# A planned two-layer metaformer kernel: layer 0's projection weights get a tile of their own, weights lie in one run a partition, and the planner lets ScalarE's and GpSimd's instructions overlap

## The chip, the cores and the metric

The kernel runs on one core of one Trainium2 chip. The metric is the device time of one execution in microseconds (us), the median of several runs. TensorE (PE) multiplies matrices, VectorE (DVE), ScalarE (ACT) and GpSimd (POOL) work element by element, and SyncE (SP) issues most of the DMAs. Each engine takes its instructions strictly in order; an instruction that waits holds up everything behind it on its engine, SP's DMA requests included.

## The reference

The input is x, 4 images of 384 channels and 32x32 positions, in float32. Two layers follow, and each has a mixing part and a feed-forward part around residual additions (cut from the reference):

```
# layer 0
x = x + L0_conv(ln_c(x))     # selective scan in 4 directions (k = 0..3)
t = tokens(x);  t = t + L0_ffn(ln_t(t))     # low-rank (Kronecker) feed-forward
# layer 1
x = x + L1_conv(ln_c(x))     # Mamba block: in_proj, causal conv of 4 taps, scan, gate, out_proj
t = tokens(x);  t = t + L1_ffn(ln_t(t))     # 4 experts, the best 2 of each token
```

A selective scan computes for each channel d and each of its 16 states n, along the positions:

```
h = exp(dt * A[d, n]) * h + dt * u * B[n]
y = sum over n of  h * C[n]
```

`dt`, `B` and `C` come from a small projection of the scan's own input. In layer 0 that projection has the weights `x_proj_weight`, 44 columns for each of the 4 directions; the kernel calls them `w_x0`. In layer 1 it is `w_x1` with 56 columns.

## The kernel before

**Scan steps.** Half an image (512 positions) in one direction, or in one half of layer 1's channels, is a pass. There are 48 passes and each has 12 steps, so 576 steps. A step covers four tiles of 128x512. For each step ACT writes the four decays `exp(dt*A)` into PSUM tiles `da` (`decay`, L1773), POOL multiplies `dt*u` by B into the tile `s` (`times_b`, L1767, one instruction of 128x2048), DVE runs four scans (`scan`, L1782), and the product with C is divided between DVE (`times_c`, L1831, one 128x512 tile each, out of PSUM) and POOL (`times_c_pool`, L1847, the last one or two tiles at once, which the scan then leaves in `s`). PE adds the states up (`add`, L1803), and after four steps DVE gathers the sum (`gather0`, L660 to L666, `gather1`, L913). There are four `s` tiles in rotation (`NSR = 4`).

**Around the scans** run the side jobs: layer norms (`layernorm`, L445 to L476), the projection of a scan's input (`prep_quad0`, L638 for layer 0, `prep_quad1`, L894 for layer 1; each serves two passes and is called a quad), the step sizes of a pass (`prep_pass`, with the stores `dts<-tmp` of L510), layer 0's feed-forward (`post0`: L710, L743, L774), layer 1's input projection and convolution (`prep1`: L793, L832), the output projection (`post1`, L952), the routing (`front`, L1070), the experts (`experts`: L1414, L1436) and the combination (`combine`: L1557, L1607). When the last scan is through, what is left of the experts runs alone; that stretch is called the tail below.

**The order is made by a planner**, the class `Plan`, when the program is built. Each piece of work states its engine and a cost in us (`yield PE, 3.2`), a DMA its engine SP and the time to its landing, `land(kb)`, which is 3.5 us and the kilobytes through 200. The planner keeps for each engine when it will be free (`free`) and for each piece when it will be done (`end`), takes the piece that can begin first by rules of `choose`, and emits its instructions. So a cost in the text moves instructions on all engines, though the chip then runs them as fast as it can. An SP request counts as 0.1 us of SP. The planner also decides, step by step, how many of the four C products DVE takes (`split`): it compares when POOL must begin the next `times_b` (`due_b`) with when it is free. Where PE has a hole in the plan, `fill` puts dummy matmuls there (L1822, 32x256).

**Tiles.** Weights of the side jobs go through four shared tiles `wts` of 128x384 (`wts.take()`, `wts.give()`). Layer 0's quad takes one of them, asks for its `w_x0` (L630) and for the `dt` weights (L631), waits in the plan for the landing and then places its matmuls:

```
wx = yield from wts.take()
yield SP, land(66)
nc.sync.dma_start(out=wx[:, :, : QROW + R0], in_=ins["w_x0"][k].rearrange("(c p) m -> p c m", p=P))
```

A quad's job begins when the quad before it is planned, and the pass that is third before its own first pass (`("pass", p - 3)`). The last thing that a pass issues is the store of `dt*u` (L510, four requests).

Of the kernel before, what the change touches and what calls it, by code (L numbers as in the profile page):

```python
# [18 lines left out]
P = 128  # L19
# [109 lines left out]
SLACK = ({PE: 0.0, DVE: 0.0, ACT: 0.0, POOL: 0.0, SP: 0.0}, {PE: 0.0, DVE: 0.0, ACT: 0.0, POOL: 0.0, SP: 0.0})  # L129
LAG = 0.15  # L130


# [32 lines left out]
class Plan:  # L165
# [66 lines left out]
    def run(self):  # L232
        while True:
# [28 lines left out]
            if isinstance(what, Lane):  # L262
                cost = what.want[1]
                self.free[e] = start + (0.1 if e == SP else cost)
                what.end = start + cost
                what.want = None
                Free.clock = what.end
                what.go(what.end, start)
            else:
                k, op = what  # L270
                self.at[e, k] += 1
                self.free[e] = start + (0.1 if e == SP else op.cost)
                self.end[op.key] = start + op.cost
                op.emit()
# [3 lines left out]
def layers(ctx, tc, ins, out, const):  # L278


    nc = tc.nc
    pvt, ident, mean_w = const["pv"], const["ident"], const["mean_w"]
    eps5, eps6, one, nil, mid = (const["few"][:, i : i + 1] for i in range(5))
    x_in = ins["x"]

# [35 lines left out]
    t1 = Free(tiles(6, [P, T], "t1"))  # L321
    wts = Free(tiles(4, [P, NC, P], "w"))


# [5 lines left out]
    slots = {u: wp.tile([P, 2, NK], I32, name=f"slot{u[0]}{u[1]}") for u in gates}  # L330
    nexts = tiles(2, [P, NE], "next", pool=wp)
    tables = [wp.tile([1, 2, pairs + lones], I32, name=f"table{s}") for s, (_, _, pairs, lones) in enumerate(STAGES)]
    since = wp.tile([P, NE], F32, name="since")
    sels = tiles(2, [P, NK + 1, NE], "sel", pool=wp)
# [60 lines left out]

    out_d = dram.tile([P, NI, D], F32, name="out_d")
    taps_d = dram.tile([NI, P, 4 * P], F32, name="taps_d")
# [82 lines left out]
    def wload(src):  # L480

        w = yield from wts.take()
        yield SP, land(192)
        nc.sync.dma_start(out=w, in_=src)
        return w
# [139 lines left out]
    def prep_quad0(q, b, k):  # L625
        def gen():
            u = st[("u0", b)]
            wx = yield from wts.take()
            yield SP, land(66)
            nc.sync.dma_start(out=wx[:, :, : QROW + R0], in_=ins["w_x0"][k].rearrange("(c p) m -> p c m", p=P))  # L630
            nc.sync.dma_start(out=dtw[dt_rows(q), :], in_=ins["w_dt0"][k])  # L631

            px = yield from ps.take(True)
            yield PE, 3.2
            for pieces in zip(*(in_order(px[h * HP : h * HP + QROW + R0], u, k, h) for h in range(NT))):
                for c in range(NC):
                    for to, of in pieces:
                        nc.tensor.matmul(  # L638
                            to, lhsT=wx[:, c, : QROW + R0], rhs=of[:, c], start=c == 0, stop=c == NC - 1
                        )  # L640
            wts.give(wx)
            for h in range(NT):
                yield ACT, 0.6
                nc.scalar.copy(xd[q["at"] : q["at"] + QROW + R0, cols(h)], px[h * HP : h * HP + QROW + R0])
            rows_out(q, slice(0, L))
            ps.give(px)

        return gen

    def prep_pass0(v, p):  # L650
# [17 lines left out]
    def post0(b, h):  # L668
# [52 lines left out]
        def ffn(lane):  # L721
            def gen():
# [6 lines left out]
                for i in range(2 * lane, 2 * lane + 2):  # L729
                    w, proj1 = yield from wts.two()  # L730
                    yield SP, land(192)
                    nc.sync.dma_start(
# [3 lines left out]
                        out=proj1[:, :, :32],  # L736
                        in_=ins["w_proj1"][i * NC * P : (i + 1) * NC * P].rearrange("(f p) i -> p f i", p=P),
                    )
# [26 lines left out]
        def ffn_out():  # L765
            zg, g = st["zg", b], st["g", b, h]
            spread = yield from wts.take()
            yield SP, land(192)
            of = spread_d.unsqueeze(0).to_broadcast([4, QP, D])
            nc.sync.dma_start(out=spread.rearrange("p a m -> p (a m)"), in_=of)  # L770
            for c in range(NC):
                ph = yield from ps.take()
                yield PE, 1.1
                nc.tensor.matmul(ph, lhsT=spread[:, c, :], rhs=g, start=True, stop=True)  # L774
                yield DVE, 0.65
                nc.vector.tensor_tensor(y[:, c], y[:, c], ph, ALU.add)
# [10 lines left out]

    w_in = ins["w_in"].rearrange("(c p) m -> p c m", p=P)
    w_out = out_d
# [5 lines left out]
    def prep1(b, h):  # L795
# [6 lines left out]
        def conv(i):  # L802
            def gen():
                for j in range(NC):
                    c = i * NC + j
                    w = yield from wload(w_in[:, :, c * P : (c + 1) * P])
                    tile_x = yield from tmp.take()
# [3 lines left out]
                    taps = [dg[:, tap * P : (tap + 1) * P] for tap in range(4)]  # L811
                    t_taps = yield SP, land(256)
                    nc.sync.dma_start(out=dg, in_=taps_d[c])
# [33 lines left out]
        def gate(i):  # L847
            def gen():
                z = yield from tmp.take()
                for j in range(NC):  # L850
                    at = (NI + i * NC + j) * P
                    w = yield from wload(w_in[:, :, at : at + P])
# [28 lines left out]
    def prep_quad1(q, b, h):  # L881
        def gen():
            wx = yield from wts.take()
            wx1 = wx.rearrange("p a m -> p (a m)")[:, : NI * (QROW + R1)].rearrange("p (c m) -> p c m", c=NI)
            yield SP, land(120)
            nc.sync.dma_start(out=wx1, in_=ins["w_x1"].rearrange("(c p) m -> p c m", p=P))
            load_dtw(q, 0)
# [27 lines left out]
    def post1(b, h, early=False):  # L915
# [23 lines left out]
        def project():  # L939
            o = st["o", b, h] = yield from tmp.take()  # L940
            for m in range(NC):
                w = yield from wts.two()
                yield SP, land(384)
                for i in range(2):
                    nc.sync.dma_start(out=w[i], in_=w_out[:, i * NC : (i + 1) * NC, m * P : (m + 1) * P])
                yield from till(lambda: all(("gated", b, h, i) in plan.end for i in range(2)))
# [57 lines left out]
    def centre():  # L1004
# [20 lines left out]
        for i in range(2):  # L1025
# [12 lines left out]
            yield SP, land(576)  # L1038
            nc.sync.dma_start(out=out_d[:, i * NC : (i + 1) * NC], in_=w)
            tmp.give(t)  # L1040
# [13 lines left out]
    def front(u):  # L1054
# [3 lines left out]
        def gen():  # L1058
# [7 lines left out]
            raw = pg[:, 192 : 192 + NK * NG1].rearrange("p (j e) -> p j e", e=NG1)  # L1066
            yield PE, 2.9
            for j in range(NK):
# [94 lines left out]

            yield PE, 1.2
            flat = sel.rearrange("p j e -> p (j e)")
# [348 lines left out]
    def combine(u):  # L1514
# [9 lines left out]
        def some(j):  # L1524
            def gen():
# [24 lines left out]
                for k in range(2):  # L1550
                    nc.scalar.activation(diag[k], ident, AF.Copy, scale=gks[u][:, k, j : j + 1])
                yield PE, 2.0, max(t + 6.0, plan.now + 1.0)
                for c in range(NC):
# [445 lines left out]
def metaformer_kernel(ctx: ExitStack, tc: tile.TileContext, ins, out):  # L1999
# [5 lines left out]
    make_identity(nc, ident)  # L2005
    mean_w = cp.tile([P, P], F32, name="mean_w")
    nc.vector.memset(mean_w, 1.0 / D)
    few = cp.tile([P, 8], F32, name="few")
    for i, x in enumerate((1e-5, 1e-6, 1.0, 0.0, 1.5)):
        nc.vector.memset(few[:, i : i + 1], x)  # L2010
    const = {"pv": pvt, "ident": ident, "mean_w": mean_w, "few": few}
    with tc.manual_schedule():
# [3 lines left out]
def _laid_out(a):  # L2016
# [12 lines left out]
    def reordered(w, rank):  # L2029

        parts = [w[..., rank + NS :, :], w[..., rank : rank + NS, :], w[..., :rank, :]]
        return np.swapaxes(np.concatenate(parts, axis=-2), -1, -2)

    pv = {
# [20 lines left out]
        "pv": np.concatenate([pv[n] for n in _PV], axis=1),  # L2055
        "w_x0": reordered(a["L0_conv_x_proj_weight"], R0),
        "w_dt0": np.swapaxes(a["L0_conv_dt_projs_weight"], 1, 2),
        "w_fc1": a["L0_ffn_c_fc_1"].T,
        "w_proj1": a["L0_ffn_c_proj_1"].T,
# [3 lines left out]
        "w_in": a["L1_conv_in_proj_w"].T,  # L2063
        "w_x1": reordered(a["L1_conv_x_proj_w"], R1),
        "w_dt1": a["L1_conv_dt_proj_w"].T,
# [27 lines left out]
```

## Time and profile before

| | us |
|---|---|
| median of 3 runs | 5031.1 (5026.45 to 5036.6) |
| the profiled execution | 5048.5 |
| its span, first instruction to last | 5046.8 |

| stretch of the span | length | PE busy | DVE busy | ACT busy | POOL busy |
|---|---|---|---|---|---|
| start, 0 to 101 | 101 | 92.3 | 32.8 | 46.4 | 10.7 |
| scan steps, 101 to 4462 | 4361 | 3676.3 | 4084.1 | 2772.0 | 3924.3 |
| tail, 4462 to 5047 | 585 | 554.0 | 43.7 | 223.4 | 43.2 |

A group line of the profile names the source line, the engine, the operation, the tiles (written<-read), the shapes and the count; after the bar come the busy time in us, the mean duration of one in ns, the idle time of the engine just before these instructions, and what ended most of it. In a line of waits the three numbers are the us in total, the times and the longest. In a timeline the first two columns are the start and the length in us; what stands in brackets is the engine's idle time before it and what ended it. An fp32 matmul shows as two records. PEclk is the granted TensorE clock as a share of full speed. Consecutive instructions of DVE, ACT and POOL overlap by some hundredths of a us in the records.

### The profile page before, as it was taken

The page shows a single profiled execution, that of the slowest core. Times are in us where ns is not written, and L with a number is a line of the kernel's source. Part 1 is how long each engine was busy: PE and PEld are TensorE (multiplying, and loading weights), DVE is VectorE, ACT ScalarE, POOL GpSimd, SP SyncE. Part 2 cuts the span into 40 slices and gives each one's busy share as a digit, 9 for nine tenths or more (in the row PEclk, how much of TensorE's full clock was granted, in tenths as well). Part 3 has the DMA queues.
Part 4 walks back from the last instruction along what each step waited for, and adds up shares of the span by engine and source line. Part 5 has one row for each costly group of instructions (what it writes and reads, how often), then busy time and mean ns, then how long its engine had stood idle before and what let it go on. Part 6 is the DMA issues. An engine that isn't in the chain of part 4 may idle for free. (4 is left out here: it accounts for less than half of the span.)

```text
span 5046.8 us, 58008 instructions
## 1 busy us (share of the span) xinstructions
PE 4322.5 (86%) x18375; PEld 2232.8 (44%) x18375; DVE 4160.7 (82%) x5795; ACT 3041.7 (60%) x4769; POOL 3978.1 (79%) x1821
## 2 busy tenths in 40 slices
PE   8877788877777899898878888889888898999997
PEld 3222222223233454344444554344533244679994
DVE  4999999989999899999998999989999899940002
ACT  4545467755544677777655577767786656644441
POOL 2999998889988888999988988989999888930002
PEclk9888898988888899999987899899998998999997
DMA  4345656643443565566655655555655456655554
GB/s 148 110 160 173 196 185 213 203 164 127 150 147 113 193 199 177 166 205 210 198 189 194 214 175 180 156 181 197 220 193 197 151 189 203 202 188 182 167 171 142
DMA packets 438163, 899.38 MB, mean 178 GB/s; under 512 B 74609, under 2 KB 187233, under 8 KB 419425
## 3 DMA queue, kind: packets, MB, share of 16 engines
q1 hardware_dynamic: 380640, 704.28, 43.3%
q10 hardware_dynamic: 49024, 166.22, 9.7%
q0 software_dynamic: 8192, 25.17, 1.5%
q8 instruction: 146, 2.39, 0.2%
q14 instruction: 161, 1.31, 0.1%
HBM read 712.11 MB, written 183.40 MB: 177 GB/s over the span
## 5 line engine op out<-in xcount | busy, mean ns | idle before, releaser
L1767 POOL TENSOR_TENSOR s<-dtus,bt 128x2048 f32<-128x2048 f32 x576 | 2607.2, 4536 | 149.9 <-PE acc L1803 81.8
L1773 ACT ACTIVATE da<-dts,a 128x512 f32<-128x512 f32 x2304 | 1529.5, 686 | 873.5 <-DVE s L1831 778.8
L1847 POOL TENSOR_TENSOR s<-s,ct 128x512 f32<-128x512 f32 (+1 forms) x547 | 911.8, 1668 | 162.7 <-DVE s L1782 118.6
L1831 DVE TENSOR_TENSOR s<-da,ct 128x512 f32<-128x512 f32 x1558 | 1029.6, 680 | 0.0
L1803 PE MATMUL acc<-s,four 128*32 128x512 f32 x4608 | 715.3, 663 | 340.4 <-POOL s L1847 299.0
L1782 DVE TENSOR_TENSOR_SCAN da<-da,state,s 128x512 f32<-128x512 f32 x771 | 960.7, 1278 | 52.3 <-ACT da L1773 51.8
L1782 DVE TENSOR_TENSOR_SCAN da<-da,s 128x512 f32<-128x512 f32 x787 | 933.8, 1216 | 77.8 <-ACT da L1773 50.1
L1822 PE MATMUL acc<-ident,few 128*32 128x256 f32 x3294 | 842.1, 410 | 43.8 <-DVE big L660 17.6
L1822 PEld LDWEIGHTS acc<-ident,few 128*32 128x32 f32 x3294 | 378.4, 118 | 582.6 <-issue 258.7
L1782 DVE TENSOR_TENSOR_SCAN s<-da,state,s 128x512 f32<-128x512 f32 x381 | 475.3, 1268 | 7.6 <-ACT da L1773 7.4
L1782 DVE TENSOR_TENSOR_SCAN s<-da,s 128x512 f32<-128x512 f32 x365 | 432.8, 1204 | 11.7 <-ACT da L1773 11.6
L1803 PEld LDWEIGHTS acc<-s,four 128*32 128x32 f32 x4608 | 105.9, 112 | 684.5 <-POOL s L1847 473.4
L1414 PE MATMUL ps<-tmp,mw 128*128 128x256 f32 (+1 forms) x1812 | 381.4, 365 | 8.1 <-DMA mw<-in_w_dram 2.0
L1414 PEld LDWEIGHTS ps<-tmp,mw 128*128 128x128 f32 x1812 | 313.3, 195 | 118.7 <-issue 32.7
L1436 PEld LDWEIGHTS ps<-mw,tmp 128*128 128x128 f32 x1968 | 331.1, 196 | 70.2 <-issue 34.9
L1436 PE MATMUL ps<-mw,tmp 128*128 128x192 f32 x1968 | 355.7, 338 | 5.6 <-DVE big L476 2.9
L1609 DVE SCALAR_TENSOR_TENSOR big<-big,gk,ps 128x384 f32<-128x384 f32 x4 | 2.4, 610 | 422.0 <-issue 422.0
L793 PE MATMUL ps<-big,w 128*128 128x512 f32 x576 | 289.5, 645 | 42.6 <-DMA w<-in_w_in_dram 29.2
L1599 POOL DMA_INDIRECT big<-ys,slot x12 | 11.4, 953 | 394.1 <-DMA ys<-t 390.7
L564 POOL TENSOR_TENSOR tmp<-tmp,big 128x256 f32<-128x256 f32 (+1 forms) x189 | 196.8, 1068 | 70.6 <-ACT tmp L551 70.5
L832 PE MATMUL ps<-tmp,t 128*128 128x512 f32 x376 | 181.2, 628 | 23.9 <-ACT tmp L824 16.3
L793 PEld LDWEIGHTS ps<-big,w 128*128 128x128 f32 x576 | 111.4, 203 | 203.1 <-issue 136.9
(461 smaller groups left out, 5407.0 us busy)
## 6 DMA issues: line engine op xcount, KB each, us to landing
mw<-in_w_dram SPq DMA_DIRECT2D x414, 384.0 KB
dts<-dts ACTq DMA_DIRECT2D x288, 512.0 KB
dtus<-dts SPq DMA_DIRECT2D x144, 1024.0 KB
dts<-tmp SPq DMA_DIRECT2D x380, 192.0 KB
bt<-rows SPq DMA_DIRECT2D x192, 256.0 KB
ct<-rows SPq DMA_DIRECT2D x192, 256.0 KB
dts<-in_w_dram SPq DMA_DIRECT2D x78, 384.0 KB
ys<-t SPq DMA_DIRECT2D x32, 768.0 KB
```

Source lines behind the costliest of these rows:

```text
L564: nc.gpsimd.tensor_tensor(to, by, u[:, c], ALU.mult)
L793: nc.tensor.matmul(pi, lhsT=w[:, c, :], rhs=u[:, c], start=c == 0, stop=c == NC - 1)
L832: nc.tensor.matmul(pk, lhsT=taps[tap], rhs=xt[:, tap : tap + T], start=tap == 0, stop=tap == 3)
L1414: nc.tensor.matmul(ph[:, k * width : (k + 1) * width], lhsT=w[:, c, k * P : (k + 1) * P], rhs=turned[:, c], start=c == 0, stop=c == NC - 1,)
L1436: nc.tensor.matmul(py[:, k * HD : (k + 1) * HD], lhsT=by_f(hids[half_], width)[:, at_, k * P : (k + 1) * P], rhs=w[:, f], start=4 * q + f ...
L1767: nc.gpsimd.tensor_tensor(ss[i % NSR], dtus[part_of(i) % 2], rep(bts[i % 4], NG), ALU.mult)
L1773: nc.scalar.activation(das[x], dts[(2 * part_of(i) + x // 2) % 3][:, x % 2, :], AF.Exp, scale=v["a"][:, g, m : m + 1])
L1782: nc.vector.tensor_tensor_scan(d if in_psum else s, d, s, 0.0 if v["first"] else state[:, v["slot"], j, x : x + 1], ALU.mult, ALU.add)
L1803: nc.tensor.matmul(acc[x * QP : (x + 1) * QP, :], lhsT=four, rhs=ss[i % NSR][:, x, :], start=m == 0, stop=m == 3)
L1822: nc.tensor.matmul(acc[:QP, : 2 * P], lhsT=nil.to_broadcast([P, QP]), rhs=rep(ident, 2), start=fresh, stop=fresh)
L1831: nc.vector.tensor_tensor(ss[i % NSR][:, x, :], das[x], cts[i % 4], ALU.mult)
L1847: nc.gpsimd.tensor_tensor(s[:, m:, :], s[:, m:, :], rep(cts[i % 4], NG - m), ALU.mult)
```

## The change

1. **Layer 0's x weights.** `w_x0` gets a tile of its own, `wx0` (128x3x44), in place of a shared `wts` tile. A new job `ask_quad0` issues the two requests (its weights and the `dt` weights), and the quad depends on that job. The ask depends on the previous quad of layer 0 and on the same pass as the quad.
2. **Layout.** `w_x0`, `w_x1`, `w_in` and `w_proj1` are laid out so that a partition's part of a load is one run; `out_d`, the prepared output weights in DRAM, is laid out so too, and is written by three requests a half instead of one.
3. **Planned costs.** A load of `w_in` and of the taps counts 2.5 us longer, of `w_fc1` 2.0, of `spread` 3.0, of `w_x1` 4.0. On PE the layer 0 quad counts 4.3 instead of 3.2, the routing matmuls 4.9 instead of 2.9 and 1.8 instead of 1.2, the combination 4.2 instead of 2.0.
4. **Overlap.** `PITCH` makes ACT free 0.07 us and POOL 0.08 us before the cost is over; `SOON` calls their results ready 0.08 and 0.05 us before it is over.
5. **Room.** `mean_w`, a tile of 128x128 that holds 1/384, becomes one column read with stride 0; `nexts` and `since` share a tile.

```
+PITCH = {PE: 0.0, DVE: 0.0, ACT: 0.07, POOL: 0.08, SP: 0.0}
+SOON = {PE: 0.0, DVE: 0.0, ACT: 0.08, POOL: 0.05, SP: 0.0}
...
-                self.free[e] = start + (0.1 if e == SP else op.cost)
-                self.end[op.key] = start + op.cost
+                self.free[e] = start + (0.1 if e == SP else op.cost - PITCH[e])
+                self.end[op.key] = start + op.cost - SOON[e]
...
+    mean_w = const["few"][:, 5:6].to_broadcast([P, P])
+    wx0 = sp.tile([P, NC, QROW + R0], F32, name="wx0")
...
-        yield SP, land(192)
-        nc.sync.dma_start(out=w, in_=src)
+        yield SP, land(192) + 2.5
+        nc.sync.dma_start(out=w.rearrange("p c m -> p (c m)"), in_=src)
...
     def prep_quad0(q, b, k):
         def gen():
             u = st[("u0", b)]
-            wx = yield from wts.take()
-            yield SP, land(66)
-            nc.sync.dma_start(out=wx[:, :, : QROW + R0], in_=ins["w_x0"][k].rearrange("(c p) m -> p c m", p=P))
-            nc.sync.dma_start(out=dtw[dt_rows(q), :], in_=ins["w_dt0"][k])
             px = yield from ps.take(True)
-            yield PE, 3.2
+            yield PE, 4.3
...
+    def ask_quad0(q, k):
+        def gen():
+            yield SP, land(66)
+            nc.sync.dma_start(out=wx0.rearrange("p c m -> p (c m)"), in_=ins["w_x0"][k])
+            nc.sync.dma_start(out=dtw[dt_rows(q), :], in_=ins["w_dt0"][k])
+        return [gen]
...
-                    yield SP, land(192)
+                    yield SP, land(192) + 2.0
...
-            yield SP, land(192)
+            yield SP, land(192) + 3.0
             of = spread_d.unsqueeze(0).to_broadcast([4, QP, D])
...
-                    t_taps = yield SP, land(256)
+                    t_taps = yield SP, land(256) + 2.5
...
-            yield SP, land(120)
-            nc.sync.dma_start(out=wx1, in_=ins["w_x1"].rearrange("(c p) m -> p c m", p=P))
+            yield SP, land(120) + 4.0
+            nc.sync.dma_start(out=wx1, in_=ins["w_x1"].rearrange("p (c m) -> p c m", c=NI))
...
-                    nc.sync.dma_start(out=w[i], in_=w_out[:, i * NC : (i + 1) * NC, m * P : (m + 1) * P])
+                    nc.sync.dma_start(out=w[i], in_=w_out[m, :, i * NC : (i + 1) * NC])
...
-            nc.sync.dma_start(out=out_d[:, i * NC : (i + 1) * NC], in_=w)
+            for m in range(NC):
+                nc.sync.dma_start(out=out_d[m, :, i * NC : (i + 1) * NC], in_=w[:, :, m * P : (m + 1) * P])
...
-            yield PE, 2.9
+            yield PE, 4.9
...
-            yield PE, 1.2
+            yield PE, 1.8
...
-                yield PE, 2.0, max(t + 6.0, plan.now + 1.0)
+                yield PE, 4.2, max(t + 6.0, plan.now + 1.0)
...
         deps = [q["need"] if layer == 0 else ("conv", b, x - 1) if x else ("post", 0, b, 0)] + ([("quad", n - 1)] if n else []) + ([("pass", p - 3)] if n > 1 else [])
+        if not layer:
+            before = [m for m in range(n) if not quads[m]["layer"]][-1:]
+            asked = [("quad", m) for m in before] + ([("pass", quads[n - 2]["p"] + 1)] if n > 1 else [])
+            jobs.append((("ask", n), asked, p, ask_quad0(q, x)))
+            deps = deps + [("ask", n)]
```

The planner sets a job's key when the job's last piece has been emitted, and the pieces of a job that was waiting for it may be placed from that moment; `land(66)` in `ask_quad0` is therefore not waited for by the quad.

More of the change, by code (lines that the diff above doesn't have):

```diff
@@ L263, in run @@
                 cost = what.want[1]
-                self.free[e] = start + (0.1 if e == SP else cost)
-                what.end = start + cost
+                self.free[e] = start + (0.1 if e == SP else cost - PITCH[e])
+                what.end = start + cost - SOON[e]
                 what.want = None
@@ L281, in layers @@
     nc = tc.nc
-    pvt, ident, mean_w = const["pv"], const["ident"], const["mean_w"]
+    pvt, ident = const["pv"], const["ident"]
     eps5, eps6, one, nil, mid = (const["few"][:, i : i + 1] for i in range(5))
+    mean_w = const["few"][:, 5:6].to_broadcast([P, P])
     x_in = ins["x"]
@@ L330, in layers @@
     slots = {u: wp.tile([P, 2, NK], I32, name=f"slot{u[0]}{u[1]}") for u in gates}
-    nexts = tiles(2, [P, NE], "next", pool=wp)
+    marks = wp.tile([P, 3, NE], F32, name="marks")
+    nexts, since = [marks[:, i] for i in range(2)], marks[:, 2]
     tables = [wp.tile([1, 2, pairs + lones], I32, name=f"table{s}") for s, (_, _, pairs, lones) in enumerate(STAGES)]
-    since = wp.tile([P, NE], F32, name="since")
     sels = tiles(2, [P, NK + 1, NE], "sel", pool=wp)
@@ L393, in layers @@
     nc.sync.dma_start(out=spread_d, in_=spread[:32, :D])
-    out_d = dram.tile([P, NI, D], F32, name="out_d")
+    out_d = dram.tile([NC, P, NI, P], F32, name="out_d")
     taps_d = dram.tile([NI, P, 4 * P], F32, name="taps_d")
@@ L638, in gen @@
                         nc.tensor.matmul(
-                            to, lhsT=wx[:, c, : QROW + R0], rhs=of[:, c], start=c == 0, stop=c == NC - 1
+                            to, lhsT=wx0[:, c, :], rhs=of[:, c], start=c == 0, stop=c == NC - 1
                         )
-            wts.give(wx)
             for h in range(NT):
@@ L736, in gen @@
                         out=proj1[:, :, :32],
-                        in_=ins["w_proj1"][i * NC * P : (i + 1) * NC * P].rearrange("(f p) i -> p f i", p=P),
+                        in_=ins["w_proj1"][i].rearrange("p (f i) -> p f i", f=NC),
                     )
@@ L785, in post0 @@
         return [ln1, [gelu, *(add_x(c) for c in range(NC))], ln2, [ffn(0), ffn(1)], ffn_out]
-    w_in = ins["w_in"].rearrange("(c p) m -> p c m", p=P)
+    w_in = ins["w_in"]
     w_out = out_d
@@ L805, in gen @@
                     c = i * NC + j
-                    w = yield from wload(w_in[:, :, c * P : (c + 1) * P])
+                    w = yield from wload(w_in[c])
                     tile_x = yield from tmp.take()
@@ L850, in gen @@
                 for j in range(NC):
-                    at = (NI + i * NC + j) * P
-                    w = yield from wload(w_in[:, :, at : at + P])
+                    w = yield from wload(w_in[NI + i * NC + j])
                     pi = yield from ps.take()
@@ L2005, in metaformer_kernel @@
     make_identity(nc, ident)
-    mean_w = cp.tile([P, P], F32, name="mean_w")
-    nc.vector.memset(mean_w, 1.0 / D)
     few = cp.tile([P, 8], F32, name="few")
-    for i, x in enumerate((1e-5, 1e-6, 1.0, 0.0, 1.5)):
+    for i, x in enumerate((1e-5, 1e-6, 1.0, 0.0, 1.5, 1.0 / D)):
         nc.vector.memset(few[:, i : i + 1], x)
-    const = {"pv": pvt, "ident": ident, "mean_w": mean_w, "few": few}
+    const = {"pv": pvt, "ident": ident, "few": few}
     with tc.manual_schedule():
@@ L2032, in reordered, with by_partition @@
         return np.swapaxes(np.concatenate(parts, axis=-2), -1, -2)
+    def by_partition(w):
+        *n, rows, width = w.shape
+        return np.swapaxes(w.reshape(*n, rows // P, P, width), -3, -2).reshape(*n, P, rows // P * width)
     pv = {
@@ L2055, in _laid_out @@
         "pv": np.concatenate([pv[n] for n in _PV], axis=1),
-        "w_x0": reordered(a["L0_conv_x_proj_weight"], R0),
+        "w_x0": by_partition(reordered(a["L0_conv_x_proj_weight"], R0)),
         "w_dt0": np.swapaxes(a["L0_conv_dt_projs_weight"], 1, 2),
         "w_fc1": a["L0_ffn_c_fc_1"].T,
-        "w_proj1": a["L0_ffn_c_proj_1"].T,
+        "w_proj1": by_partition(np.stack(np.split(a["L0_ffn_c_proj_1"].T, 4))),
         "c_proj_2": np.tile(a["L0_ffn_c_proj_2"].reshape(-1), 32),
@@ L2062, in _laid_out @@
         "c_mask_t": mask.T,
-        "w_in": a["L1_conv_in_proj_w"].T,
-        "w_x1": reordered(a["L1_conv_x_proj_w"], R1),
+        "w_in": by_partition(np.stack(np.split(a["L1_conv_in_proj_w"].T, 2 * NI, axis=1))),
+        "w_x1": by_partition(reordered(a["L1_conv_x_proj_w"], R1)),
         "w_dt1": a["L1_conv_dt_proj_w"].T,
```

## The prediction

> **What bounds the kernel now.** I read the windows by stage first. The columns after the length are busy us (and instructions) of PE, its weight loads, DVE, ACT and POOL.
>
> ```profile
> 101.00:4462.00 4361.00, 3676.26 (x15176) 1723.63 (x15175) 4084.10 (x5501) 2771.99 (x4313) 3924.27 (x1764) 0.90 0.55 180
> 4462.00:5047.00 585.00, 553.99 (x2907) 470.82 (x2906) 43.73 (x126) 223.35 (x379) 43.17 (x44) 0.94 0.55 169
> ```
>
> While steps run, DVE is busy 4084 of 4361 us, and its 277 us of idle time are what better order could win. POOL has 437 us free. The tail is PE's. Next the groups by form show what DVE and POOL share:
>
> ```profile
> L1767 POOL TENSOR_TENSOR s<-dtus,bt 128x2048 f32<-128x2048 f32 x576 | 2607.2, 4536 | 149.9 <-PE acc L1803 81.8 <-issue 42.1 <-DMA dtus<-dts 19.2
> L1847 POOL TENSOR_TENSOR s<-s,ct 128x1024 f32<-128x1024 f32 x199 | 468.9, 2359 | 91.7 <-DVE s L1782 75.7 <-DVE t L1177 2.6 <-PE acc L1803 2.1
> L1847 POOL TENSOR_TENSOR s<-s,ct 128x512 f32<-128x512 f32 x348 | 442.9, 1273 | 71.0 <-DVE s L1782 42.9 <-DVE t L1131 5.2 <-DVE ps L1124 3.5
> ...
> L1831 DVE TENSOR_TENSOR s<-da,ct 128x512 f32<-128x512 f32 x1558 | 1029.6, 680 | 0.0
> L1797 DVE COPY state<-da 128x1 f32<-128x1 f32 x787 | 115.0, 146 | 0.0
> ```
>
> Then the waits say who stops whom. DVE's largest wait is for decays that ACT wrote late; ACT in turn stands behind the copy of layer 0's quad (L644), and that behind weights:
>
> ```profile
> DVE da L1782 <- ACT da L1773: 102.0, 48, 10.4
> ACT xd L644 <- PE ps L638: 95.6, 14, 12.5
> PE ps L638 <- DMA w<-in_w_x_dram: 55.2, 9, 8.6
> PE ps L793 <- DMA w<-in_w_in_dram: 29.2, 9, 7.5
> ```
>
> The timeline of one quad shows the chain. SP stands 7.11 us at the stores of the pass before, asks for the weights only then, they land 2.4 us later, PE had idled 8.60 us, ACT's copy comes last, and DVE loses 7.10 us:
>
> ```profile
> 1293.57 7.11 SPq L510 DMA_DIRECT2D dts<-tmp  x4
> ...
> 1300.72 0.43 SPq L630 DMA_DIRECT2D w<-in_w_x_dram  x1
> ...
> 1303.13 5.27 PE L638 MATMUL ps<-big,w 128*44 128x512 f32 x12 [8.60 <-DMA w<-in_w_x_dram]
> ...
> 1308.44 0.58 ACT L644 COPY xd<-ps 44x512 f32<-44x512 f32 x1 [11.61 <-PE ps L638]
> ...
> 1309.64 1.29 DVE L1782 TENSOR_TENSOR_SCAN da<-da,state,s 128x512 f32<-128x512 f32 x1 [7.10 <-ACT da L1773]
> ```
>
> Last I followed each DVE gap of over 0.4 us in the scan steps (259 us in all) back in the timeline to what had held the chain up. Layer 0 quads: 53 us. Loads of `w_in` and the taps: 27; of `spread`: 17; of `w_fc1`: 9; matmuls of the combination: 14; of the routing: 9; the `w_x1` quad: 5. The rest (ACT's table loads, decays, adds, layer norms, 125 us) is not touched by name.
>
> **Part 1, the overlap (PITCH, SOON): −21 us.** The built order of the changed kernel has 1529 C products on DVE instead of 1558 and 775 state copies instead of 787, because the planner sees POOL free earlier. By the groups above one costs 1029.6/1558 = 0.661 us and one copy 115.0/787 = 0.146, so DVE sheds 29 x 0.661 + 12 x 0.146 = 20.9 us. POOL gets 24 more of the 1024 form and 19 fewer of the 512 form: 24 x 2.359 − 19 x 1.273 = +32 us, inside its 437 free us. So the move is worth 21 us as long as DVE is the bound; if POOL were, it would cost 32. A rule speaks against it: the Trainium skill, "GPSIMD Engine Reference", section 3.1, keeps elementwise work on VectorE, since GpSimd takes 1.96 times as long. The trace agrees on the ratio (1273 against 680 ns, 1.87 times); by the rule alone 29 tiles would lose 29 x 0.593 = 17 us, and it decides only where POOL is late.
>
> The new figures are nearer to the trace: two decays take 1.30 us together where one takes 0.69, and after a 1.27 us product POOL begins the next 1.23 us later. But the old ones left ACT and POOL a hidden margin. DVE waits for decays 63 times (121 us). If each waits longer by the 0.08 of SOON and four PITCHes of 0.07, that is 63 x 0.36 = 23 us; if the truer figures help, 0 or a gain of as much. I take +8, nearer to none, since DVE runs 6% behind its own work anyway, which gives ACT and POOL time.
>
> **Part 2, truer costs for loads and matmuls: −54 us.** The planner thought 4.5 us for a `w_in` load; the waits in the timeline show 2.7 to 8.8 from request to use, for `spread` 4.8 to 9.8, for `w_fc1` 2.9 to 9.2. New entries are 7.0, 7.5 and 6.5. The routing's 24 matmuls took 5.2 us, planned 2.9, now 4.9. What these edits cover is 27 + 17 + 9 + 14 + 9 + 5 = 81 us of DVE's idle time. All of it could go (−81); none, if the later places only shift the waits (0). A later matmul delays its ACT copy by the same plan, so some comes back: I take two thirds, −54.
>
> **Part 3, the `w_x0` tile: +24 us.** The request is no longer in the quad's own job, so the quad's matmuls wait in the plan for the request's emission and not for its landing. The built program numbers its instructions in the planner's order. Between request and first matmul lay 3.6 to 7.5 us of DVE instructions in the old order at the 14 quads after the first two; in the new one no DVE instruction lies between them at eight quads, and 1.2 us at a ninth. There the request still follows the stores (L510), whose four issues take SP 2.2 us at the least (7.11 above), because both hang on the same pass. So PE reaches the quad about 3.8 us sooner and waits for the same landing. The longer PE cost (4.3 for 3.2) gives 1.1 us of it back to ACT and the adds: net 2.7 us a quad, 9 x 2.7 = +24. DVE's gaps at these nine are now 4.9, 3.2, 3.8, 2.2, 7.1, 2.9, 9.6, 6.4 and 5.5, sum 46. At the others the request goes out 3 to 67 us ahead; what is won there is about 3 us at one (10.8 now) and lies in part 2 elsewhere. Bounds: −25 if the shorter runs and the free tile bring the requests forward after all, +42 if all 3.8 us and 0.9 of adds behind count.
>
> The one-run layout makes a `w_x0` run 528 bytes instead of 176. Request to use took 2.3 to 4.3 us at eleven quads. [...]
>
> **With one answer: 0.** The first scan (100.9 us) waits for stores of pass 0; four more requests for `out_d` at 0.34 to 0.76 us stand before them on SP, half of them in the way (+1), while the first quad comes forward by some 1 us, where 21 dummy matmuls stood in its way. The tail holds the same instructions by kind and count but for 18 dummies of 95, so its 585 us stay. Stride-0 weights cost what others do (118 ns, L1822, against 112, L1803, for 32 columns). 204 fewer dummies of 2 x 0.2 us lie in PE's holes; what they covered is PE's clock (0.90 granted), which bounds only the tail.
>
> **Sum.** −21 + 8 − 54 + 24 = −43 us. The profiled execution took 5048.5 us (span 5046.8), 17.4 above the median; the change would bring it to 5005, and the median of 5031.1 to 4988.
>
> **Rivals.**
>
> *The unplanned landing decides (slower).* One mechanism: at nine quads PE stands in front of weights not yet asked for, behind it the adds, behind those DVE's gathers and POOL's ring. If each of the nine then costs what the worst costs now, 10.8, and 3.8 more, they take 131 us instead of 46: +85, and the sum is −21 + 8 − 54 + 85 = +18, so 5049. It decides from (21 − 8 + 54)/9 = 7.4 us more a quad. For it: PE idled 8.3 and 8.6 us at two of them, and quads of 512-column matmuls took 5.3 us after such idling and 2.8 without. Against it: at four the gap was under 3.5 us.
>
> *Nothing arrives (same).* The freed 21 us become waits of DVE for POOL or ACT, and the truer costs move waits without removing them: −21 + 23 = +2, 5033. For it: most gaps are ACT's, and ACT is in order. Against it: DVE's wait for POOL after the start is under 3 us.
>
> *Nearly all covered stalls go (much faster).* −21 − 81 − 10 = −112, the last term for quads a little earlier than now: 4919. For it: the waits name exactly the edited lines. Against it: part 3.
>
> **How the numbers follow.** Forecast 0.47, slower rival 0.26, same 0.12, much faster 0.15. The forecast's own bounds reach from −21 − 81 + 0 = −102 (all covered stalls go, quads as now) to −21 + 23 − 20 + 42 = +24 (a quarter of them go, every other term at its worst), that is 4929 to 5055; with the rivals' outer halves the range that leaves 2 in 10 out is 4915 to 5065. A measurement of this kernel tells about 0.2% (10 us) from no change. Faster: 0.47 + 0.15 = 0.62; same 0.12; slower 0.26.
>
> **What would show it.** Right: L1831 falls to 1529 records and 20 us less busy; DVE's busy time in the steps is near 4063 and its idle time near 255; `PE <- DMA w<-in_w_in_dram` and `spread_d` nearly vanish from the waits; `PE L637 <- DMA wx` grows above 80 us, with gaps of DVE at those quads. Wrong: waits for `wx` gone (part 3 has the wrong sign), waits of DVE for POOL above 20 us (part 1), the tail off 585 by more than 5.

## The result and the profile after

The changed kernel takes 5042.6 us (median of 21 runs) beside 5032.8 of the kernel before on the same chip (21 runs): the ratio is 1.0017, 95% interval 1.001 to 1.0025, so some 8.5 us slower where 43 faster were predicted.

The windows by stage (columns as before: length, busy us of PE, its weight loads, DVE, ACT, POOL):

```profile
99.00:4478.00 4379.00, 3627.28 (x14813) 1691.00 (x14813) 4082.97 (x5460) 2767.76 (x4313) 3951.85 (x1770) 0.88 0.54 179
4478.00:5031.00 553.00, 545.63 (x2869) 465.17 (x2868) 43.11 (x126) 223.38 (x379) 44.41 (x44) 0.96 0.59 179
```

The steps grew by 18 us with DVE's busy time unchanged, so the loss is idle time of DVE. The tail's 32 us less are mostly no gain: the profiled execution of before held waits of PE of 27 us in its last combination, 21.1 of them in one piece, that this one lacks. They go with the chip or the execution and not with the change: in all eight profiles below from the two chips on which the kernel before takes 5055 us, PE waits 22 to 26 us there, and in the other ten, from chips with 5030 to 5034, under 3.5. So most of the 17.4 us by which the profile of before stood above its median may well be this wait, and steps, not spans, are compared between profiles below.

The groups that Part 1 spoke of:

```profile
L1778 POOL TENSOR_TENSOR s<-dtus,bt 128x2048 f32<-128x2048 f32 x576 | 2605.3, 4533 | 178.1 <-PE acc L1814 67.2 <-issue 62.4 <-DMA dtus<-dts 39.8
L1858 POOL TENSOR_TENSOR s<-s,ct 128x1024 f32<-128x1024 f32 x223 | 524.7, 2355 | 78.1 <-DVE s L1793 66.0 <-DMA mw<-in_w_dram 1.9 <-POOL s L1778 1.6
L1858 POOL TENSOR_TENSOR s<-s,ct 128x512 f32<-128x512 f32 x329 | 417.8, 1270 | 60.5 <-DVE s L1793 36.0 <-DVE t L1137 5.8 <-DVE ps L1130 3.7
L1842 DVE TENSOR_TENSOR s<-da,ct 128x512 f32<-128x512 f32 x1529 | 1009.6, 680 | 0.1
```

DVE has 1529 products and spends 20.0 us less on them, as predicted; still it is as busy as before. The waits, over the whole span:

```profile
ACT xd L642 <- PE ps L637: 106.8, 14, 15.7
PE ps L637 <- DMA wx<-in_w_x_dram: 93.8, 12, 14.9
DVE da L1793 <- ACT da L1784: 92.5, 39, 14.1
DVE big L666 <- PE acc L1814: 47.1, 20, 7.6
DVE big L918 <- PE acc L1814: 31.6, 17, 8.3
PE ps L799 <- DMA w<-in_w_in_dram: 8.2, 2, 5.8
DVE big L782 <- PE ps L780: 5.3, 6, 2.1
DVE tmp L1568 <- PE ps L1563: 3.9, 5, 1.7
```

The stalls that Part 2 named went for the most part: `w_in` 29.2 to 8.2, `spread` 17.3 to 5.3, the combination 23.7 to 3.9. But the quad's wait for its weights grew from 55.2 to 93.8, and DVE's gathers wait longer for the adds: over the four gather lines 90.7 us in the steps, 58.7 before. The quad with the longest gap shows how (timeline; SP is still at the stores of L514 when PE already stands):

```profile
1664.21 8.83 SPq L514 DMA_DIRECT2D dts<-tmp  x4
...
1673.09 0.43 SPq L651 DMA_DIRECT2D wx<-in_w_x_dram  x1
...
1675.43 5.41 PE L637 MATMUL ps<-big,wx 128*44 128x256 f32 x24 [12.04 <-DMA wx<-in_w_x_dram]
...
1680.88 0.58 ACT L642 COPY xd<-ps 44x512 f32<-44x512 f32 x1 [15.65 <-PE ps L637]
...
1683.57 2.35 DVE L1793 TENSOR_TENSOR_SCAN da<-da,s 128x512 f32<-128x512 f32 x2 [14.12 <-ACT da L1784]
```

The weights land 2.3 us after the request, but PE had been in front of them for 12.0 us, and DVE loses 14.1. At the nine quads with no lead DVE's gaps within 12 us of the quad's first copy sum to 79 us, 46 before; within 8 us they sum to 74, and 46.

### The profile page after: what moved, and what is told of

Read it like the earlier page. It is cut to its first block, busy times and chain, and to the rows that moved or that the text cites. A ratio compares the mean times of both kernels' runs of the same rounds, so it can differ in the third digit from the quotient of the medians.

```text
span 5031.0 us, 57132 instructions
## 1 busy us (share of the span) xinstructions
PE 4262.9 (85%) x17967; PEld 2192.9 (44%) x17967; DVE 4159.0 (83%) x5754; ACT 3037.3 (60%) x4769; POOL 4006.4 (80%) x1826
## 5 line engine op out<-in xcount | busy, mean ns | idle before, releaser
L1814 PE MATMUL acc<-s,four 128*32 128x512 f32 x4608 | 735.1, 682 | 382.0 <-POOL s L1858 344.9
L1858 POOL TENSOR_TENSOR s<-s,ct 128x512 f32<-128x512 f32 (+1 forms) x552 | 942.5, 1708 | 138.6 <-DVE s L1793 102.0
L1842 DVE TENSOR_TENSOR s<-da,ct 128x512 f32<-128x512 f32 x1529 | 1009.6, 680 | 0.1
L1793 DVE TENSOR_TENSOR_SCAN da<-da,state,s 128x512 f32<-128x512 f32 x754 | 939.5, 1277 | 17.7 <-ACT da L1784 10.1
L1833 PE MATMUL acc<-ident,few 128*32 128x256 f32 x2886 | 751.5, 416 | 36.2 <-DVE big L918 18.6
L1833 PEld LDWEIGHTS acc<-ident,few 128*32 128x32 f32 x2886 | 334.4, 119 | 510.6 <-issue 225.1
L1793 DVE TENSOR_TENSOR_SCAN s<-da,state,s 128x512 f32<-128x512 f32 x398 | 495.5, 1267 | 8.7 <-ACT da L1784 8.6
L1793 DVE TENSOR_TENSOR_SCAN s<-da,s 128x512 f32<-128x512 f32 x377 | 447.1, 1204 | 17.3 <-ACT da L1784 17.3
L1442 PE MATMUL ps<-mw,tmp 128*128 128x192 f32 x2096 | 377.1, 337 | 17.5 <-DMA mw<-in_w_dram 6.8
L1442 PEld LDWEIGHTS ps<-mw,tmp 128*128 128x128 f32 x2096 | 350.4, 195 | 82.4 <-issue 42.9
L529 PE MATMUL ps<-xd,dtw 12*128 12x512 f32 (+1 forms) x288 | 187.9, 743 | 17.2 <-ACT tmp L542 9.4
```

Source lines behind the costliest of these rows:

```text
L529: nc.tensor.matmul(pd, lhsT=dtw[dt_rows(q), c * P : (c + 1) * P], rhs=xd[dt_rows(q), cols(h)], start=True, stop=True,)
L1442: nc.tensor.matmul(py[:, k * HD : (k + 1) * HD], lhsT=by_f(hids[half_], width)[:, at_, k * P : (k + 1) * P], rhs=w[:, f], start=4 * q + f ...
L1793: nc.vector.tensor_tensor_scan(d if in_psum else s, d, s, 0.0 if v["first"] else state[:, v["slot"], j, x : x + 1], ALU.mult, ALU.add)
L1814: nc.tensor.matmul(acc[x * QP : (x + 1) * QP, :], lhsT=four, rhs=ss[i % NSR][:, x, :], start=m == 0, stop=m == 3)
L1833: nc.tensor.matmul(acc[:QP, : 2 * P], lhsT=nil.to_broadcast([P, QP]), rhs=rep(ident, 2), start=fresh, stop=fresh)
L1842: nc.vector.tensor_tensor(ss[i % NSR][:, x, :], das[x], cts[i % 4], ALU.mult)
```

## Experiments

All ratios are to the kernel before, measured beside it on the same chip. One short name for each kernel.

**The change in four parts.** *Overlap alone*, *costs alone*, *tile alone*, *layout alone*: each is the kernel before with one part of the change (the last two also carry its room edits). (The kernel *tile alone* counted its quad at 4.3 us; the text on record says 3.2 in error, and by the ledger 24 us are the measure for it.)

> The kernel before with PITCH and SOON alone; its plan has 36 C products fewer on DVE. Ledger of the prediction (DVE sheds its work, a small loss of margin): 36 x 0.66 = 24 us less DVE work, some 8 us more waits for ACT, so about 16 us faster (ratio 0.997). Rival, the freed time becomes waits: DVE busy falls by 20 us in the steps, its idle time rises by as much, ratio 1.000 +- 0.002. If the hidden margin in ACT's and POOL's costs was worth more than thought, slower: ratio up to 1.003, with DVE's waits for decays up by more than 20 us.

> The kernel before with the longer planned costs of loads and matmuls alone (not the quad's 4.3). Ledger: two thirds of 81 us of covered stalls go, 54 us faster (ratio 0.989). Rival, the stalls move: the waits for w_in and spread go, but gathers wait for the adds behind the matmuls that now come later, and the ratio is 0.998 to 1.002.

> The kernel before with the own tile and the asking job alone (old layout in DRAM, the quad at its old cost of 3.2 us). Ledger: 3.8 us more idle time at nine quads, about 34 us slower (ratio 1.007), and the wait of the quad's matmul for its weights grows to above 100 us in all. Rival, the quads are covered and the loss lies elsewhere: ratio 0.999 to 1.002 with the wait as large.

> The kernel before with the one-run layouts and the stride-0 mean weights alone; the plan stays as it was. Ledger: 0, to at most 2 us less at each of 14 quads (ratio 0.995 to 1.000). Rival, the layout costs: three requests for each half of the prepared weights and columns read with stride 0 make it slower, ratio above 1.001.

| kernel | ratio | 95% | us |
|---|---|---|---|
| overlap alone | 1.0013 | 1.0002 to 1.0024 | +7 |
| costs alone | 0.9904 | 0.9887 to 0.9921 | −48 |
| tile alone | 1.0121 | 1.0105 to 1.0136 | +61 |
| layout alone | 0.9999 | 0.9987 to 1.0011 | −1 |

The layout is worth nothing that could be measured, although packets fall from 438,163 to 394,194. The costs bring nearly what was predicted (−54). In their profile the largest of their stalls, 29.2 us at `w_in`, is nearly gone:

```profile
L793 PE MATMUL ps<-big,w 128*128 128x512 f32 x576 | 288.7, 643 | 7.3 <-DMA w<-in_w_in_dram 5.3
```

But not all of the time came as the prediction said, from DVE's idle time. Beside *layout alone*, which has the old plan and ran on the same chip, the profile of *costs alone* is 53 us ahead when pass 44 starts and only 24 after the last scan. Some 30 us go at the start of pass 46, and the gathers of layer 1 wait longer (*layout alone* has 4.3 and 19.5 us at these two):

```profile
DVE big L558 <- ACT ps L556: 25.5, 4, 22.9
DVE big L913 <- PE acc L1803: 38.5, 12, 10.3
```

DVE's idle time between the first scan and the last is 264 us, 284 in *layout alone*: 21 of the 39 us between these two profiles. The rest lies in DVE's work (3), ahead of the first scan (6) and in the tail (9). So its rival, that stalls move, is partly seen too.

The overlap took 28 us of work from DVE (4056 us busy in the steps; some 9 of the 28 are the routing's small instructions, below), and DVE idled 328 us, where *layout alone* idles 284. The waits say where; the first three are from the overlap, the next three from *layout alone*:

```profile
DVE big L662 <- PE acc L1805: 29.9, 18, 7.3
DVE big L915 <- PE acc L1805: 29.4, 15, 6.0
POOL s L1769 <- PE acc L1805: 105.4, 48, 9.3
```

```profile
DVE big L664 <- PE acc L1807: 25.1, 11, 8.5
DVE big L916 <- PE acc L1807: 19.5, 14, 6.6
POOL s L1771 <- PE acc L1807: 82.4, 42, 8.5
```

The gathers, and POOL's next `times_b`, wait for PE's adds. Of DVE's 44 us more, the gathers are 22 (84 for 62, all four lines), waits for POOL 11 and the routing's waits for its matmuls 10. The waits for decays, where the prediction had put the lost margin, stayed (126 us for 125). Why the adds come later was not tried.

**The landing put back, and the early request.** *Landed* is the changed kernel with one wait in the plan:

```
+            plan.end["wx", q["n"]] = plan.now + land(66)     # in ask_quad0
+            yield "at", plan.end["wx", q["n"]]               # in prep_quad0, before the matmuls
```

*Early* asks for `wx0` as soon as the quad before is done and waits in the plan for that landing; only the request for `dtw` waits for the pass. *Early without overlap* sets PITCH and SOON to zero.

```
-            asked = [("quad", m) for m in before] + ([("pass", quads[n - 2]["p"] + 1)] if n > 1 else [])
+            asked = [("quad", m) for m in before]
...
-            nc.sync.dma_start(out=dtw[dt_rows(q), :], in_=ins["w_dt0"][k])    # in ask_quad0; now in prep_quad0
-            yield PE, 4.3
+            yield PE, 4.3, max(plan.now, plan.end["wx", q["n"]])
```

> The changed kernel, and the quad waits in the plan for the landing of its weights again (same tile, same request). If the missing landing is what lost the gain, what is left is overlap, costs and layout, 1.0013 + 0.9904 - 1 = 0.992 of before, the wait of the quad's matmul for wx falls from 94 us to below 60, and the gathers' waits for the adds from 91 us to about 60. Rival, the three parts get in each other's way wherever the quads stand: ratio 0.998 to 1.002, gathers still near 90.

> The changed kernel, and wx0 is asked for as soon as the quad before is done, without a pass in between; only the dt weights still wait for the pass. The plan puts 19 to 600 us of DVE work between request and quad instead of 0 to 67. If the late request is the cost of a quad, waits for wx vanish, and of the 71 us of DVE gaps at 14 quads of before most go: 0.992 less 40 to 70 us, ratio 0.978 to 0.984. Rival, the quad's matmuls are late for other reasons (adds queued behind 12 matmuls, the clock after idling): no better than with the landing planned, 0.992.

> The same early request, and PITCH and SOON at zero. If the overlap costs what it did alone (ratio 1.0013), this is 0.001 below the early request with overlap. By the prediction's ledger (19 to 24 us less DVE work with it) it is 0.002 to 0.004 above.

Measured: landed 0.9926 (0.9909 to 0.9942), early 0.9881 (0.9862 to 0.990), early without overlap 0.9913 (0.9896 to 0.993). One missing wait in the plan costs 0.0091, 46 us. In the profile of *landed* the gaps at the nine quads are 47.5 us, nearly as in before; the quads' wait for `wx` fell to 61.5, the gathers' waits only to 79. (The granted clock in the steps is 0.90 in before and *landed*, 0.88 in the changed kernel, 0.89 in *early*; no run separates what that costs, but the quad below takes the same 5.41 us as above.) With the early request PE waits for weights at no quad of layer 0, and the quad above becomes this (the waits for `wx` are gone from the profile):

```profile
1620.39 3.36 SPq L514 DMA_DIRECT2D dts<-tmp  x4
...
1625.60 5.41 PE L639 MATMUL ps<-big,wx 128*44 128x256 f32 x24
...
1631.05 0.58 ACT L644 COPY xd<-ps 44x512 f32<-44x512 f32 x1 [3.30 <-PE ps L639]
```

The gaps at the nine fall to 15 us. The gain over *landed* is 23 us, less than the 40 to 70 expected. One profile of each does not show where it lies: their steps are equally long (4323 us) with 237 us of idle time in *landed* and 239 in *early*, so in these two what the quads win is lost elsewhere. With the early request the overlap is worth 16 us (0.9913 to 0.9881), near the 13 of the prediction's ledger and unlike the overlap alone.

**Less work on DVE by another way.** *LAG 14*: the kernel before with `LAG = 0.14`.

> The kernel before with LAG at 0.14 instead of 0.15: no cost of a side job changes, but the plan moves 62 C products from DVE to POOL (1497 for 1559). If DVE's work is the time, 62 x 0.66 = 41 us faster (ratio 0.992). If the moved work comes back as waits, as in the kernel with the overlap alone (28 us less DVE work, 55 us more idle time against one run of before): ratio 1.000 to 1.006, with DVE's idle time 40 to 70 us larger.

Measured 0.9901 (0.9882 to 0.992): DVE 4043 us busy, 41 less, and idle 278. (The trace has 1477 products on DVE for 1558, so 81 moved; the text on record says 62 in error.) Here DVE's work is the time. So the overlap's failure is not that DVE had ceased to be the bound. The same with the early request:

> The changed kernel with the early request (0.9881) and LAG 0.14 (alone 0.9901; 82 more C products go from DVE to POOL). If DVE's work stays the time: 0.9881 - 0.0099 = 0.978. Rival, POOL becomes the bound: 0.985 to 0.995, with DVE's waits for POOL above 40 us in the steps and POOL's idle time below 300 us.

Measured 0.9891 (0.9875 to 0.9907), no better than *early*: DVE is 67 us less busy (4017) and 69 us more idle (309). Its waits for POOL in the steps are 82 us for 16, and POOL's own idle time is 275: the signs of the rival, that POOL becomes the bound. What is moved beyond a point comes back as idle time.

**Nudges.** How much of a price is one plan's luck? LAG 0.151 for 0.150 in four kernels, and the tile alone with the landing.

> A change that means nothing: the kernel before with LAG 0.151 instead of 0.150. It puts 9 more C products on DVE (6 us by the ledger). If the time of a plan follows from its parts, ratio 0.999 to 1.002. Rival, the planner's order is chaotic and any nudge throws the side jobs of the last passes about: ratio off 1 by 0.003 or more, to either side, with the difference in passes 36 to 47.

> The same nudge on the changed kernel (LAG 0.151): the requests of the quads stand as in it, nine with no lead. If the loss is in the nine quads and not in the luck of one order, ratio 0.998 to 1.005 of the kernel before, as the changed kernel's 1.0017, and 0.006 or more above the kernel with the landing planned (0.9926). Rival, luck of order: below 0.997 or above 1.006.

> The kernel before with own tile, asking job and quad cost 4.3, and the quad waiting in the plan for the landing. Against the same without that wait (1.0121): if the missing landing costs 5 us and more at each quad, 46 to 61 us come back, ratio 1.000 to 1.003. Rival, what that kernel lost is in the last passes, where no quad is: the ratio stays above 1.006.

> The own tile and asking job alone as before (1.0121), with LAG 0.151. If the price of the missing landing belongs to it: 1.009 to 1.015, with the loss again partly in passes 36 to 47, where no quad of layer 0 is. If two thirds of it were the luck of that one order: 1.001 to 1.007.

> The overlap alone (1.0013), with LAG 0.151. That kernel's profile is 47 us ahead of its counterpart with the same layout of plan at pass 29 and loses 53 us after it. If the late loss belongs to the overlap: 1.000 to 1.003 again, with the same turn. If it was the luck of one order: 0.993 to 0.998.

| kernel | ratio | nudged |
|---|---|---|
| before | 1 | 1.0010 (0.9996 to 1.0023) |
| after | 1.0017 | 1.0018 (1.0008 to 1.0028) |
| overlap alone | 1.0013 | 1.0006 (0.9993 to 1.002) |
| tile alone | 1.0121 | 1.0028 (1.0018 to 1.0038) |
| tile alone, landed | 0.9996 (0.9986 to 1.0007) | |

Three kernels hardly move; the tile alone moves by 47 us. So of its 61 us some 14 are left after the nudge, and the rest goes with the order of one plan. The place agrees: against *tile alone, landed* it lost 13 us in passes 0 to 7, won 11 up to pass 35 and lost 35 in passes 36 to 47, where no quad of layer 0 runs. The loss of the changed kernel itself holds under the nudge. *Landed*, *early* and the two kernels below were built in one order each and not nudged.

**The parts taken out of the change.**

> The changed kernel with PITCH and SOON at zero (costs, tile and layouts as changed). Prediction's ledger: the overlap is worth 13 us, so this is 1.0017 + 0.0026 = 1.004. By the overlap alone (1.0013) it is 1.000 to 1.001. By the pair with the early request (0.9881 with, 0.9913 without): 1.005.

> The changed kernel with the old costs of loads and matmuls (overlap, tile, quad cost 4.3 and layouts as changed). If the longer costs are worth inside the change what they were alone (0.9904): 1.0017 + 0.0096 = 1.011. Rival, they are worth less beside the late quads: 1.002 to 1.007.

Without overlap 1.0095 (1.0079 to 1.0112), without costs 1.014 (1.0121 to 1.0159): inside the change the overlap is worth 39 us and the costs 62, both more than any text on record expected. The parts don't add. What the overlap does there is not a lighter DVE (4080 us busy without it, 4083 with it). I summed DVE's gaps between the last scan of a pass and the first of the next: 6 us in before, 48 after, 104 without the overlap. Of the 104, 67 lie at the start of pass 46, in the last half image of layer 1, and 24 at pass 26. The two longest at pass 46:

```profile
4310.27 0.69 DVE L562 TENSOR_TENSOR tmp<-tmp,ps 128x512 f32<-128x512 f32 x1 [19.94 <-ACT ps L560]
...
4350.92 1.29 DVE L1793 TENSOR_TENSOR_SCAN da<-da,state,s 128x512 f32<-128x512 f32 x1 [31.53 <-ACT da L1784]
```

L562 is a step of that pass's own `prep_pass`: its inputs were not ready when pass 45 ended. *Costs alone* idles there too (22.9 us in one piece), the changed kernel 13.8 in several, before not. All kernels that idle over 12 us at this place have the longer load costs or LAG 0.14; why the overlap shortens it was not tried.

**What held DVE's small instructions.** The 20 us that left L1842's group did not lower DVE's busy time mostly because the routing's instructions (those of `front` and `blocks`, up to the last scan) took 134.7 us instead of 119.2. The timelines of before, DVE first, then POOL:

```profile
2686.83 0.16 DVE L1112 TENSOR_TENSOR t<-t 128x4 f32<-128x4 f32 x1
2687.03 1.27 DVE L1113 TENSOR_SCALAR t<-t 128x4 f32<-128x4 f32 x1
2688.33 4.41 DVE L1114 TENSOR_TENSOR t<-t 128x4 f32<-128x4 f32 x1
```

```profile
2687.00 1.27 POOL L1847 TENSOR_TENSOR s<-s,ct 128x512 f32<-128x512 f32 x1
2688.23 9.00 POOL L1767 TENSOR_TENSOR s<-dtus,bt 128x2048 f32<-128x2048 f32 x2
```

L1113 ends with POOL's first product, L1114 with half of the next pair. All 18 routing instructions of over 1 us in before, and all 19 after, end within 0.04 us of the end of an instruction of POOL. *Small in PSUM* gives the five lines and the cast of the slots one operand or result in PSUM, in before and in *early*:

```
+            nc.scalar.copy(r_ps, r)
-            nc.vector.tensor_scalar(var, var, 1.0 / D, 1e-5, ALU.mult, ALU.add)
-            nc.vector.tensor_tensor(a, r, r, ALU.mult)
+            nc.vector.tensor_scalar(var_ps, var, 1.0 / D, 1e-5, ALU.mult, ALU.add)
+            nc.vector.tensor_tensor(a, r_ps, r, ALU.mult)
...
```

> The kernel before; of the routing's five small DVE instructions on 128x4 (L1110 to L1114) and the cast of the slots each now has an operand or its result in PSUM, which costs one copy of 128x4 on ACT. In before these six lines take 40 us more than their undisturbed 0.15 to 0.17 us each would, and every routing instruction of over 1 us ends with an instruction of POOL. If they wait for POOL because they use SBUF alone: none of them over 0.5 us, DVE's busy time in the steps down by 35 to 40 us, ratio 0.992 to 0.996. Rival, they wait for something else that POOL holds, or the freed time becomes idle: durations or the time unchanged, ratio 0.998 to 1.002.

> The same edit on the changed kernel with the early request (0.9881), where these lines take 50 us more than undisturbed. If DVE's busy time is the time: 0.9881 - 0.009 = 0.979 to 0.983. If the freed time becomes idle time at the borders of passes and at gathers: 0.986 to 0.989.

Measured 0.9928 (0.9911 to 0.9944) and 0.9811 (0.9796 to 0.9827). The same instruction by its durations (ns, minimum, median, maximum), before and with the edit:

```profile
L1114 DVE TENSOR_TENSOR t<-t x7: 161/161/4412, 1416.0 to 4373.7; 128x4 f32<-128x4 f32 x7
```

```profile
L1114 DVE TENSOR_TENSOR ps<-t,ps x7: 166/166/168, 1407.8 to 4341.3; 128x4 f32<-128x4 f32 x7
```

(L1114 is another of the five in the second, the product with the variance; all five and the cast stay under 0.17 us there, though 37 of their 42 records in the steps begin while POOL runs an instruction.) DVE's busy time in the steps fell by 40 us and nearly all of it came as time. The second kernel, the changed one with the early request and small tiles in PSUM, is the best here: 4939.3 us, 91 under before, 0.9811.

## Why the prediction was wrong

**Part 3 had the right mechanism and was mis-sized.** +24 predicted, 46 measured for the missing landing. The step that failed is "net 2.7 us a quad, 9 x 2.7 = +24", which lets the longer PE cost give 1.1 of the 3.8 us back and has no term for the plan outside these quads. At the nine quads the gaps grew from 46 us to 74 or 79, so by 3.1 to 3.7 us each: little of the 1.1 came back, and this is inside the bound of +42. The other 13 to 18 us lie outside the nine. One profile of each kernel shows 13.8 us at the start of pass 46 in the changed kernel and none in *landed*, which is near but not a proof, since *landed* is one order of the plan.

**Part 1 failed where it stands alone.** −21 + 8 = −13 predicted, +7 and +3 measured. The work did leave DVE, but it came back as idle time: the term for lost margin was +8 and measured some 35 (28 us less work, 7 us more time). It was looked for only at the decays, whose waits did not move; half of it stood at the gathers behind PE's adds. Beside the early request the same edit won 16 us and inside the change 39, so it has no one price. The Trainium skill's "GPSIMD Engine Reference", section 3.1, advises against moving elementwise work to GpSimd; the overlap alone (36 products moved, 7 us lost) agrees with it, and *LAG 14* (81 moved, 50 us won) does not.

**Part 2 came in by its number, by its mechanism in part.** −54 predicted, −48 alone (−62 inside the change). The named stalls mostly went, as the waits said. But of the 53 us won in the steps up to pass 44, 29 were lost behind it, most of them at the start of pass 46, a wait that the ledger did not know; some 15 us came from the start and the tail, where it had counted nothing. So that the sum came out so near is partly luck.

**The sum.** With +5 for the overlap alone, −48 and +46 it is +3, beside the measured +8.5 with an interval of 5 to 13. By this account Parts 1 and 3 hold 18 + 22 us of the 51 that were missed and Part 2 holds 6. It is one account of several: taken out of the change, overlap and costs are worth 39 and 62. What needs no adding is that the changed kernel with the landing put back is 46 us faster than without it.

**The rivals.** *The unplanned landing decides* had the sign. Its price of 14.6 us of gap a quad was too high (79/9 = 8.8 measured), and the 7.4 us more a quad from which it decides were not reached at 3.1 to 3.7, or 5.1 with all of the 46. Its 5049 and the 5033 of *Nothing arrives* lie 9 and 7 us from the 5040 that 1.0017 of 5031 makes; of the latter the first half came true for the overlap alone, the second did not, since the costs won 48 us. The layout, for which up to 2 us a quad had been expected, gave 1 us in all.

**What would show it.** `wx` above 80: yes, 93.8. `w_in` and `spread` nearly gone: yes. L1842 20 us less: yes. DVE 4063 busy and 255 idle: no, 4083 and 296; the first by the small instructions, the second by quads and pass starts. Waits of DVE for POOL above 20 us, as a sign of being wrong: not reached, 15 in the steps. The tail was off by 32, mainly by the waits in before's last combination and 18 dummies fewer (18 x 2 x 0.21 = 8 us).

## What to carry to other kernels

A planned wait is part of the data flow: where a request moves into another job, see that its consumer still waits in the plan for the landing (here −37 us instead of +8.5), and ask for it a whole stage earlier where you can (−60). Work moved off the bound engine need not be a gain: sum what is freed and look at the idle time it returns as, and nudge the plan before you believe the price of one order. And before summing a stretch's busy time, look at the spread of the smallest instructions: a median of 0.16 us with a maximum of 4.4 is a wait, not work.

## What the runs showed of the hardware

A DVE instruction on 128x4 numbers, all in SBUF, that started while POOL ran an instruction mostly ended with that one or with the next: 0.16 us became up to 9.6. With one operand or the result in PSUM, six such lines stayed under 0.17 us in 42 records, 37 of them begun while POOL ran. The Trainium skill, "SBUF — State Buffer", section "Who interferes with whom", says that a DVE instruction with two SBUF inputs contends with a GpSimd instruction that reads SBUF, and that a DVE instruction in its two-port mode, which `tensor_scalar` and casts can enter, and GpSimd lock each other out for a whole instruction. The trace agrees, and shows the price: some 40 us of DVE in a kernel whose routing takes only 119.

One-run loads (528 bytes for 176 in `w_x0`, 44,000 packets fewer in all) made no difference that could be measured: 0.9999 (0.9987 to 1.0011).
